# The first and the last group of a two-layer graph attention set apart: TensorE transposes at both ends, and the last output projection graph by graph

## Chip, cores, metric

The kernel runs on one core of one Trainium2 chip. The metric is the device time of one execution in microseconds. The runs of one kernel lie within some 0.3% of each other. "Span" is the time from the first to the last instruction in a profile; it is 1.5 to 2 us shorter than the device time of the same run. TensorE is called PE in the profile (PEld its weight loads), VectorE DVE, the scalar engine ACT, GpSimd POOL, and the DMA-issuing engine SP.

## The reference, cut to what matters

There are 128 graphs of 128 nodes with 512 features, all float32, and two attention layers with 8 heads.

```python
# layer 0                                             # layer 1
Q, K, V = x@W_q+b_q, x@W_k+b_k, x@W_v+b_v             q, k, v = x@Wq.T+bq, x@Wk.T+bk, x@Wv.T+bv
s = Q K^T / sqrt(64) + a_i + c_j + log(adj + 1e-9)    s = q k^T / sqrt(64) + log(clip(adj, 1e-8))
x = softmax(s) V + x                                  out = (softmax(s) v) @ Wo.T + bo
                                                      result = layer_norm(x + out) * gamma + beta
```

The initial gamma is all ones and beta all zeros.

## The kernel before

Four graphs form a group, and 32 groups pass through two layers, so there are 64 steps t. The products with the weights are one level of Strassen (seven products, P1 to P7, of four 128x256 matmuls each), computed in the order P1, P2, P6, P5, P7, P3 and P4 moved in between products of the next matrix. P6, P5 and P7 need sums of x (T1 to T4, made by GpSimd) and sums of the weights (S1 to S4, the "combine", made by VectorE). Work is put into numbered slots between the products; the order of the slots is the order of each engine's instructions in the program. In the profile's names p0, p1 and p2 are the PSUM banks into which TensorE writes the products, and the last letter is the matrix (P6 of V is `p0v<-wv,T`, P5 `p2v<-wv,T`); s are the scores, av the products with V, o the scalar engine's copy of av, aT its transpose, po the output projection, h what is normalised and stored. A record is one entry of the trace; a float32 matmul leaves two (four matmuls show as x8).

The matmuls take x transposed (`xT` in their records). It is loaded in 32x32 blocks; the DMA places the blocks and VectorE's stream transpose turns each block (0.71 us a graph):

```python
    load_tiles(0)
    strassen_weights(WV, 0, w_v0, "wv0", nc.scalar)
    load_graph(0, 0, nc.sync)       # 4 transfers of 64 KB each
    load_graph(0, 1, nc.sync)
    load_graph(0, 2, nc.scalar)
    load_graph(0, 3, nc.scalar)
    load_natural(0)                 # the same x again, as it lies, for the residual
    strassen_weights(WQ, 0, w_q0, "wq0", nc.scalar)
    strassen_weights(WK, 0, w_k0, "wk0", nc.scalar)
    load_adjacency(0, nc.sync)
    Strassen.combine(nc.vector, WV[0])
    for b in range(G):
        turn(XT[0][:, b])
```

The last group's output projection stands after everything else. Its operand is moved by DMA in blocks and turned by VectorE, for two graphs at a time:

```python
    for k in range(2):
        put(post, a + 5 + 4 * k, move, t, k, [nc.sync, nc.scalar] if k else [nc.sync])   # 16 transfers
    ...                                       # all slots run here
    for k in range(2):
        for b in (2 * k, 2 * k + 1):
            turn(AT[t][:, b])
        for b in (2 * k, 2 * k + 1):
            output(b)                         # 4 matmuls of 128x512, sum, statistics, scaling
            if b:
                finish(b - 1)                 # times gamma, plus beta, store
    finish(G - 1)
```

## Time and profile before

| | before |
|---|---|
| median of 3 runs | 3506.12 us (3505.57 to 3507.63) |
| span of the profiled run (another one, 3504.51 us) | 3502.7 us |
| PE busy | 3453.6 us |
| third product (P6) starts | 23.45 us |
| first scores' product of group 0 starts | 61.27 us |
| first scores' product of the last group starts | 3433.96 us |
| last instruction of any engine ends | 3496.6 us |

Read it by its two ends. Between the first scores' product and that of the last group TensorE has no gap to speak of (the longest between its records is 0.17 us), so any gain must come from before 61 us or after 3434 us. The prediction shows the lines.

### The profile page before, as it was taken

How to read it: one execution, taken by the hardware profiler on the slowest of the kernel's cores; microseconds unless marked ns; L12 is line 12 of the kernel's file. 1: busy time of each engine (PE TensorE's matmuls, PEld its weight loads, DVE VectorE, ACT ScalarE, POOL GpSimd, SP SyncE). 2: the span in 40 equal slices, each digit the busy share in tenths (PEclk: the TensorE clock that was granted, in tenths of full speed). 3: DMA queues.
4: the chain of work that ended last, by engine and by line, in shares of the span. 5: the costliest groups of instructions: out<-in, count | busy, mean ns of one | idle time of the engine just before them, and what ended most of it. 6: DMA issues, size and time to landing. Idle time of an engine off the chain costs nothing. (4 is left out here: it accounts for less than half of the span.)

```text
span 3502.7 us, 54508 instructions
## 1 busy us (share of the span) xinstructions
PE 3453.6 (99%) x20730; PEld 3080.4 (88%) x20730; DVE 1769.9 (51%) x2813; ACT 1203.0 (34%) x2333; POOL 1574.0 (45%) x987
## 2 busy tenths in 40 slices
PE   8999999999999999999999999999999999999996
PEld 7888888888888888888888888888888888888884
DVE  4555555555555555554444444545444444444443
ACT  2333333333333333333333333333333333333332
POOL 2333233333233333254555555555555555555554
PEclk9999999999999999999999999999999999999998
DMA  5332323332323332342333434242423333333432
GB/s 130 73 76 70 76 61 79 73 77 70 75 61 79 73 77 71 86 98 46 70 84 65 90 62 92 60 95 58 85 67 74 79 71 83 68 87 64 91 61 76
DMA packets 1036087, 265.33 MB, mean 76 GB/s; under 512 B 961840, under 2 KB 969008, under 8 KB 1035824
## 3 DMA queue, kind: packets, MB, share of 16 engines
q1 hardware_dynamic: 1026160, 257.86, 33.1%
q10 hardware_dynamic: 9664, 3.93, 0.5%
q8 instruction: 168, 2.75, 0.3%
q14 instruction: 95, 0.78, 0.1%
HBM read 160.97 MB, written 67.11 MB: 65 GB/s over the span
## 5 line engine op out<-in xcount | busy, mean ns | idle before, releaser
L99 PEld LDWEIGHTS av<-v,e 128*128 128x128 f32 x4096 | 537.3, 191 | 28.3 <-ACT o L99 1.8
L99 POOL TENSOR_TENSOR xn<-o,xn 128x1024 f32<-128x1024 f32 x64 | 148.8, 2324 | 862.6 <-DVE o L99 578.3
L99 PE MATMUL av<-v,e 128*128 128x65 f32 x4096 | 513.3, 268 | 1.4 <-ACT o L99 1.4
L99 DVE TENSOR_TENSOR e<-e,adjT 128x1024 f32<-128x1024 f32 x256 | 352.3, 1417 | 142.7 <-ACT e L99 142.7
L99 ACT COPY o<-av 128x260 f32<-128x260 f32 x512 | 192.6, 376 | 604.8 <-PE av L99 596.9
L99 POOL TENSOR_TENSOR xn<-xn,bo 128x1024 f32<-128x1024 f32 x64 | 153.6, 2419 | 368.5 <-DMA xn<-x1d 368.4
L99 POOL TENSOR_TENSOR T<-xT 128x512 f32<-128x512 f32 x128 | 208.7, 1631 | 188.2 <-DMA xn<-in_x_dram 105.0
L99 PE MATMUL p1v<-wv,T 128*128 128x256 f32 x1128 | 273.4, 385 | 0.0
L99 DVE SCALAR_TENSOR_TENSOR junk<-xn,wg 128x512 f32<-128x512 f32 x256 | 272.0, 1062 | 0.0
L99 PE MATMUL p0q<-T,wq 128*128 128x256 f32 x1128 | 268.3, 381 | 0.0
L99 PE MATMUL p1k<-T,wk 128*128 128x256 f32 x1128 | 266.5, 379 | 0.0
L99 PE MATMUL s<-qT,kT 64*128 64x128 f32 x4096 | 263.1, 278 | 0.0
L99 PEld LDWEIGHTS s<-qT,kT 64*128 64x128 f32 x4096 | 238.6, 188 | 25.6 <-issue 21.2
L99 DVE STREAM_TRANSPOSE xT<-xT 128x512 f32<-128x512 f32 x256 | 176.5, 700 | 156.8 <-DMA xT<-x1d 150.9
L99 PEld LDWEIGHTS p1k<-T,wk 128*128 128x128 f32 x1128 | 214.3, 190 | 29.1
L99 PEld LDWEIGHTS p0q<-T,wq 128*128 128x128 f32 x1128 | 211.7, 190 | 27.4
L99 PEld LDWEIGHTS p1v<-wv,T 128*128 128x128 f32 x1128 | 205.7, 190 | 25.4
L99 POOL TENSOR_TENSOR h<-h,xn 128x1024 f32<-128x1024 f32 x62 | 174.6, 2817 | 75.0 <-DVE h L99 75.0
L99 DVE TENSOR_TENSOR qT<-p2q,u3q 128x512 f32<-128x512 f32 x64 | 44.3, 692 | 312.3 <-ACT u3q L99 312.3
L99 ACT ACTIVATE e<-s,c 128x1024 f32<-128x1024 f32 x128 | 135.9, 1113 | 142.1 <-PE s L99 142.1
L99 PE MATMUL p0o<-wo,T_o 128*128 128x256 f32 x744 | 182.4, 388 | 0.0
L99 ACT ACTIVATE e<-s 128x1024 f32<-128x1024 f32 x128 | 124.1, 1021 | 142.1 <-PE s L99 142.1
(145 smaller groups left out, 6425.8 us busy)
## 6 DMA issues: line engine op xcount, KB each, us to landing
xn<-in_x_dram SPq DMA_DIRECT2D x64, 512.0 KB, 4.2
x1d<-xn SPq DMA_DIRECT2D x64, 512.0 KB, 3.0
xT<-x1d SPq DMA_DIRECT2D x512, 64.0 KB, 2.6
xn<-x1d SPq DMA_DIRECT2D x64, 512.0 KB, 6.3
aT<-o SPq DMA_DIRECT2D x1016, 32.0 KB, 2.0
xT<-in_x_dram SPq DMA_DIRECT2D x504, 64.0 KB, 2.7
out_dram<-h SPq DMA_DIRECT2D x62, 512.0 KB, 4.2
adjT<-in_adj_dram SPq DMA_DIRECT2D x256, 64.0 KB, 2.5
```

The lines of the kernel that those rows point to most:

```text
L99: return lambda *args, **kw: self.tc.keep_in_program_order(f(*args, **kw))
```

## The change

The intent is to take the block loads and block turning off the two places where nothing hides them. In the first group x is loaded only as it lies, ahead of the rest, and TensorE transposes it against an identity; wq and wk move to the sync queue. In the last group each graph is normalised, transposed on TensorE, projected and finished by itself, in the slots between the last products with V. The group before the last gets its statistics and scaling half by half, and VectorE takes gamma and beta of its second half over from GpSimd.

```diff
-    load_graph(0, 0, nc.sync) ... load_graph(0, 3, nc.scalar)
+    load_natural(0)
     strassen_weights(WV, 0, w_v0, "wv0", nc.scalar)
-    load_natural(0); strassen_weights(WQ ..., nc.scalar); strassen_weights(WK ..., nc.scalar)
     load_adjacency(0, nc.sync)
+    strassen_weights(WQ ..., nc.sync); strassen_weights(WK ..., nc.sync)
+    make_identity(nc, ident)
+    def transposed(dst, src, name, copy):
+        p = ps.tile([P, KC, N], F32, tag="s", bufs=2, ...)
+        for c in range(KC):
+            nc.tensor.transpose(p[:, c], src[:, c * P : (c + 1) * P], ident)
+        copy(dst, p)
+    for b in range(G):
+        transposed(XT[0][:, b], XN[0, b // 2][:, b % 2], ..., nc.vector.tensor_copy if b % 2 else nc.scalar.copy)
     Strassen.combine(nc.vector, WV[0])
-    for b in range(G):
-        turn(XT[0][:, b])
 ...
+                else:                                    # the group before the last
+                    for n in range(2):
+                        put(post, o - 1 + n, residual, t, n)
+                        ... stats, scales of this half at o + 1 + 2 * n
+                    ends = o + 2, o + 4
+                for n in range(2):
+                    put(post, ends[n], scale, t, 2 * n)
+                    put(post, ends[n], scale, t, 2 * n + 1)
+                    put(post, ends[n] + (t == LAST - 2), store, t, n, nc.vector if t == LAST - 2 and n else nc.gpsimd)
 ...
-    (move by DMA, turn, output and finish of the last group, as above)
+    for b in range(G):
+        put(post, a + 3 + 2 * b, normalise_one, b)
+        put(pre, a + 5 + 2 * b, transpose_one, b)
+        put(pre, a + 6 + 2 * b, output_one, b)
+        put(pre, a + 8 + 2 * b, finish_one, b)           # (h - mean) * rs; * gamma; + beta; store
```

More of the change, by code (lines that the diff above doesn't have):

```diff
@@ L425, in scale, with store @@
         nc.scalar.activation(h, h, AF.Identity, scale=rs[:, 0, b : b + 1], bias=rs[:, 1, b : b + 1])
-    def store(t, n):
+    def store(t, n, engine):
         _, g = split(t)
-        nc.gpsimd.tensor_tensor(HS[t, n], HS[t, n], wide(GA), ALU.mult)
-        nc.gpsimd.tensor_tensor(HS[t, n], HS[t, n], wide(BE), ALU.add)
+        engine.tensor_tensor(HS[t, n], HS[t, n], wide(GA), ALU.mult)
+        engine.tensor_tensor(HS[t, n], HS[t, n], wide(BE), ALU.add)
         nc.sync.dma_start(
@@ L452, in fast_path @@
     load_tiles(0)
+    load_natural(0)
     strassen_weights(WV, 0, w_v0, "wv0", nc.scalar)
-    load_graph(0, 0, nc.sync)
-    load_graph(0, 1, nc.sync)
-    load_graph(0, 2, nc.scalar)
-    load_graph(0, 3, nc.scalar)
-    load_natural(0)
-    strassen_weights(WQ, 0, w_q0, "wq0", nc.scalar)
-    strassen_weights(WK, 0, w_k0, "wk0", nc.scalar)
-    load_adjacency(0, nc.sync)
+    load_adjacency(0, nc.sync)
+    strassen_weights(WQ, 0, w_q0, "wq0", nc.sync)
+    strassen_weights(WK, 0, w_k0, "wk0", nc.sync)
+    ident = const.tile([P, P], F32, name="ident")
+    make_identity(nc, ident)
+    def transposed(dst, src, name, copy):
+        p = ps.tile([P, KC, N], F32, tag="s", name=f"tr_{name}", bufs=2, padded_shape=[P, 2 * KC, N])
+        for c in range(KC):
+            nc.tensor.transpose(p[:, c], src[:, c * P : (c + 1) * P], ident)
+        copy(dst, p)
+    for b in range(G):
+        transposed(XT[0][:, b], XN[0, b // 2][:, b % 2], f"x_{b}", nc.vector.tensor_copy if b % 2 else nc.scalar.copy)
+    TS[0] = quarters(XT[0])
     Strassen.combine(nc.vector, WV[0])
-    for b in range(G):
-        turn(XT[0][:, b])
-    TS[0] = quarters(XT[0])
     for s in Strassen.SUMS:
@@ L516, in fast_path @@
         put(pre, a + 3, scores, t, 1)
-        put(post, a + 5, normalise, t, 0)
-        put(post, a + 9, normalise, t, 1)
-        put(post, a + 9, count, t)
+        if t + 1 < LAST:
+            put(post, a + 5, normalise, t, 0)
+            put(post, a + 9, normalise, t, 1)
+            put(post, a + 9, count, t)
         if t:
@@ L555, in fast_path @@
                 o = slot("o", t, "P3")
-                for i, n in ((0, 1), (1, 0)):
-                    put(post, o + i, residual, t, n)
-                for i, b in enumerate((0, 1, 2, 3)):
-                    put(post, o + 3 + i, stats, t, b)
-                put(post, o + 6, scales, t, slice(0, G))
-                for i in range(2):
-                    put(post, o + 8 + i, scale, t, 2 * i)
-                    put(post, o + 8 + i, scale, t, 2 * i + 1)
-                    put(post, o + 8 + i, store, t, i)
+                if t < LAST - 2:
+                    for i, n in ((0, 1), (1, 0)):
+                        put(post, o + i, residual, t, n)
+                    for b in range(G):
+                        put(post, o + 3 + b, stats, t, b)
+                    put(post, o + 6, scales, t, slice(0, G))
+                    ends = o + 8, o + 9
+                else:
+                    for n in range(2):
+                        put(post, o - 1 + n, residual, t, n)
+                        for b in (2 * n, 2 * n + 1):
+                            put(post, o + 1 + 2 * n, stats, t, b)
+                        put(post, o + 1 + 2 * n, scales, t, slice(2 * n, 2 * n + 2))
+                    ends = o + 2, o + 4
[3 more added lines that the diff above has]
+                    put(post, ends[n] + (t == LAST - 2), store, t, n, nc.vector if t == LAST - 2 and n else nc.gpsimd)
     V1, V2 = slot("v", NG - 1, "P1"), slot("v", NG, "P1")
@@ L583, in fast_path @@
     a = slot("k", t, "P3") + 2
-    WR = {}
+    last = {}
     def plain_weight():
-        WR[0] = weights.tile([P, KC, D], F32, tag="w", name="wo_plain")
-        nc.sync.dma_start(WR[0], w_o1t.rearrange("(c p) e -> p c e", p=P))
-    put(post, slot("v", t, "P3"), plain_weight)
-    end = 7 * len(mats) + 3
-    for k in range(2):
-        put(post, a + 5 + 4 * k, move, t, k, [nc.sync, nc.scalar] if k else [nc.sync])
-    for i in range(-1, max(max(pre), max(post), end) + 1):
+        last["w"] = weights.tile([P, KC, D], F32, tag="w", name="wo_plain")
+        nc.sync.dma_start(last["w"], w_o1t.rearrange("(c p) e -> p c e", p=P))
@@ new lines, in prepare, with normalise_one @@
+    def prepare():
+        last["o"] = act.tile([P, G, D], F32, tag="xT", name="o_last", bufs=2)
+        AT[t] = act.tile([P, G, KC, N], F32, tag="aT", name="aT_last")
+        h = act.tile([P, G, D], F32, tag="xT", name="h_last", bufs=2)
+        HS[t, 0], HS[t, 1] = h[:, 0:2], h[:, 2:4]
+        RC[t] = small.tile([P, G, 2, KC], F32, tag="rc", name=f"rc_{t}", bufs=3)
+    def normalise_one(b):
+        o = OR[t, b // 2][:, b % 2]
+        rc = RC[t][:, b].rearrange("p s c -> p (s c)")
+        nc.vector.reciprocal(rc, o[:, :, HD])
+        nc.vector.tensor_tensor(
+            last["o"][:, b].rearrange("p (h d) -> p h d", d=HD), o[:, :, 0:HD],
+            rc.rearrange("p (h o) -> p h o", o=1).to_broadcast([P, H, HD]), ALU.mult,
+        )
@@ new lines, in transpose_one, with output_one @@
+    def transpose_one(b):
+        transposed(AT[t][:, b], last["o"][:, b], f"o_{b}", nc.scalar.copy if b % 2 else nc.vector.tensor_copy)
+    def output_one(b):
+        p = ps.tile([P, D], F32, tag=f"p{b % 3}", name=f"po_{t}_{b}")
+        for c in range(KC):
+            nc.tensor.matmul(p, AT[t][:, b, c], last["w"][:, c], start=(c == 0), stop=(c == KC - 1))
+        h = HS[t, b // 2][:, b % 2]
+        nc.vector.tensor_tensor(h, p, XN[t, b // 2][:, b % 2], ALU.add)
+        stats(t, b)
+        rs = RS[t][:, 0, b : b + 1]
+        nc.gpsimd.tensor_scalar_add(rs, MV[t][:, b, 1:2], LN_EPS)
+        nc.gpsimd.tensor_tensor(rs, rs, minus_half[:, b : b + 1], ALU.pow)
@@ new lines, in finish_one @@
+    def finish_one(b):
+        h = HS[t, b // 2][:, b % 2]
+        nc.vector.tensor_scalar(h, h, MV[t][:, b, 0:1], RS[t][:, 0, b : b + 1], ALU.subtract, ALU.mult)
+        nc.vector.tensor_tensor(h, h, GA, ALU.mult)
+        nc.vector.tensor_tensor(h, h, BE, ALU.add)
+        nc.sync.dma_start(out[split(t)[1] * G + b], h)
+    put(post, slot("v", t, "P3"), plain_weight)
+    put(post, a, prepare)
+    for b in range(G):
+        put(post, a + 3 + 2 * b, normalise_one, b)
+        put(pre, a + 5 + 2 * b, transpose_one, b)
+        put(pre, a + 6 + 2 * b, output_one, b)
+        put(pre, a + 8 + 2 * b, finish_one, b)
@@ L595, in fast_path @@
+    put(post, a + 9, count, t)
+    for i in range(-1, max(max(pre), max(post), 7 * len(mats) + 3) + 1):
         for u in pre.get(i, []):
@@ L600, in fast_path @@
             u()
-    for k in range(2):
-        HS[t, k] = work.tile([P, 2, D], F32, tag="h", name=f"h_{t}_{k}")
-    def output(b):
-        p = ps.tile([P, D], F32, tag=f"p{b % 3}", name=f"po_{t}_{b}")
-        for c in range(KC):
-            nc.tensor.matmul(p, AT[t][:, b, c], WR[0][:, c], start=(c == 0), stop=(c == KC - 1))
-        nc.vector.tensor_tensor(HS[t, b // 2][:, b % 2], p, XN[t, b // 2][:, b % 2], ALU.add)
-        stats(t, b)
-        scales(t, slice(b, b + 1))
-        scale(t, b)
-    def finish(b):
-        h = HS[t, b // 2][:, b % 2]
-        nc.vector.tensor_tensor(h, h, GA, ALU.mult)
-        nc.vector.tensor_tensor(h, h, BE, ALU.add)
-        nc.sync.dma_start(out[split(t)[1] * G + b], h)
-    for k in range(2):
-        for b in (2 * k, 2 * k + 1):
-            turn(AT[t][:, b])
-        for b in (2 * k, 2 * k + 1):
-            output(b)
-            if b:
-                finish(b - 1)
-    finish(G - 1)
 def layer_norm(nc, small, h, GA, BE, minus_half, name):
```

## The prediction

> **What bounds the kernel now.** I read the page's busy rows first, then the waits of TensorE, then windows over the two ends, then the order of instructions in time at each end, and last the chain that ended last.
>
> ```profile
> PE 3453.6 (99%) x20730; PEld 3080.4 (88%) x20730; DVE 1769.9 (51%) x2813; ACT 1203.0 (34%) x2333; POOL 1574.0 (45%) x987
> ...
> PE   8999999999999999999999999999999999999996
> ```
>
> TensorE is busy 99% of the span, and only the first and the last of the 40 slices are not full. So the kernel's length is TensorE's work plus what it stands idle at the ends. The waits say the same: four long ones carry nearly all of it.
>
> ```profile
> PE po L99 <- DVE aT L99: 17.1, 2, 13.4
> PE p0v L99 <- DVE xT L99: 11.5, 1, 11.5
> PE sums_total L662 <- DVE sums_ones L660: 6.8, 1, 6.8
> PE p0v L99 <- ACT t1v L99: 6.0, 1, 6.0
> ```
>
> The first and third are at the end, the second and fourth at the start. Windows over the ends (PE busy first, granted clock third from last):
>
> ```profile
> 18.40:23.40 5.00, 0.00 (x0) 0.00 (x0) 3.40 (x3) 1.87 (x2) 4.07 (x3) 0.95 1.16 286
> 23.40:30.00 6.60, 6.55 (x24) 5.61 (x25) 3.88 (x5) 0.59 (x1) 1.92 (x4) 0.78 0.90 215
> 30.00:87.00 57.00, 57.00 (x337) 50.86 (x336) 31.06 (x57) 18.98 (x38) 12.64 (x8) 1.00 0.42 83
> 3451.00:3469.00 18.00, 3.70 (x28) 3.15 (x27) 8.84 (x17) 4.43 (x8) 8.96 (x7) 0.66 0.28 47
> ```
>
> From 30 us on TensorE has no gap at all; in the 18 us from 3451 it works 3.7. The start in order of time:
>
> ```profile
> 18.45 0.71 DVE L99 STREAM_TRANSPOSE xT<-xT 128x512 f32<-128x512 f32 x1 [4.64 <-DMA wq<-in_L_gnn_W_q_dram]
> 19.25 1.26 POOL L99 TENSOR_TENSOR T<-xT 128x512 f32<-128x512 f32 x1 [18.81 <-DVE xT L99]
> ...
> 23.45 3.36 PE L99 MATMUL p0v<-wv,T 128*128 128x256 f32 x8 [5.97 <-ACT t1v L99]
> ...
> 26.64 1.89 PE L99 MATMUL p2v<-wv,T 128*128 128x256 f32 x8
> ```
>
> The fourth graph's x is turned only at 18.45 (the releaser named is wq, but what the instruction needs is the x load, issued on the same queue). GpSimd's sums T1 and T2 follow, then the third product, P6, at 23.4. In front of it only two products (P1, P2) have run, 3.4 us at the later pace of 1.72 us a product. The end in order of time:
>
> ```profile
> 3454.98 17.29 SPq L99 DMA_DIRECT2D aT<-o  x24
> ...
> 3468.74 1.31 DVE L99 STREAM_TRANSPOSE aT<-aT 128x512 f32<-128x512 f32 x2 [6.67 <-DMA aT<-o]
> 3469.51 9.22 PE L99 MATMUL po<-wo_plain,aT 128*128 128x512 f32 x16 [13.41 <-DVE aT L99]
> ...
> 3482.38 7.13 PE L99 MATMUL po<-wo_plain,aT 128*128 128x512 f32 x16 [3.65 <-DVE aT L99]
> ...
> 3496.49 0.14 DVE L663 TENSOR_SCALAR bad<-sums_total 1x1 int32<-1x1 f32 x1 [0.37 <-PE sums_total L662]
> ```
>
> The last product with V ends at 3456.1; the rows moved by DMA (32 transfers of 32 KB) hold the output projection back until 3469.5; the last instruction of any engine ends at 3496.6. So 40.5 us pass after the last product with V.
>
> [...] records of a 128x256 product take 634 ns at 11.5 us and 379 ns from about 15 us, and after the gap P6 needs 3.0 us where the next product needs 1.72. [...] o<-o,rc (128x1024) takes 1226 ns alone and 3311 ns beside GpSimd's residual; the four combines of wq take 5.67 us beside GpSimd's sums, those of wv alone 2.62.
>
> **The start, part by part.** Removed: 16 loads of x in 32x32 blocks (9.31 us of issuing on one queue and 9.91 on the other, which also held back the scalar engine's table load to 21.4 and with it the copy t1v) and four stream transposes. Added: 16 TensorE transposes and four copies out of PSUM; the identity is built by GpSimd, which is idle until x lands. The natural-layout x is loaded anyway; it moves to the front and costs two issues of 0.57 us.
>
> I work it out so. x (1 MB) and wv (1 MB) now go first, together. The slices of the DMA at the start show about 300 GB/s once running, from about 2 us: half of it, the first xn tile and half of wv, is there at 2 + 1.05 MB / 300 = 5.5, landed at about 6.3; all at about 9.3. A transpose I take at 0.25 us at full clock and 0.5 at half, from the 128x65 products with V (four in 1.00 us[...]): 1 to 2 us per graph. Graphs 0 and 1: 6.3 to about 9.5. Graphs 2 and 3: to about 12.5 (11 if one pass suffices, 14.3 if all stays cold). VectorE's copy of graph 3, 0.69: 13.2. GpSimd's T1 and T2, 1.3 each: 15.9. The combine of wv, which ran early before and now stands behind the copies, needs two operations for S2, 1.3 us alone and 2.8 beside GpSimd: 14.5 to 16. P1 and P2 run from 12.5, half cold, about 4.5 us: 17.0. So P6 starts at about 17.0, warm, and the product after it at 18.7 instead of 26.4. **Gain at the start: 7.7 us** (5.4 to 9.2). wq is needed at 22.2; it is issued on the one queue from about 7 and lands near 14. The loads of the second group move forward about as much as TensorE does, as the queue has 8 issues of x fewer.
>
> **The end, part by part.** I place everything on the clock of the kernel before. Up to av of graph 1 nothing moves. Graph 0 is normalised at 47.7 to 48.6 (3400 left off), transposed at 48.6 to 49.6, but its copy into aT waits for the last Strassen product that reads the old aT, which the transpose pushes to 51.3: copy 51.5 to 52.2, projection 52.3 to 54.0 (four matmuls of 0.43, warm). The two engines that set the rest are VectorE and, once, the scalar engine. The scalar engine has the scaling of the previous group's h ahead of the copy of av of graph 3; it waits for VectorE's statistics (57.9) and GpSimd's four small ones (1.7): 59.6, then two scales of 0.73 and the copy. As av has one bank, TensorE waits from 58.7 to about 61.7. Then transpose of graph 2 to 63.7, its copy 64.5, projection to 66.3; graph 3's transpose 67.3, copy behind another scaling 68.1, projection 69.8.
>
> VectorE is later than that. It has, after 63.8, copy 0.7, normalise 0.85, count 0.45, finish of graph 1 (0.5 + 1.4 + 1.4, beside GpSimd's gamma and beta of the previous group): 69.1; sum and statistics of graph 2, 1.5: 70.6; gamma and beta of 128x1024, which it took over from GpSimd, 1.7 + 1.2: 73.6; finish of graph 2, 1.9: 75.5; sum and statistics of graph 3, 1.5: 77.0; GpSimd's two small ones (0.9 to 1.7): 78.2; finish of graph 3, 1.9: 80.1; the good-count as before 0.84: 81.0. Before: 96.6. **Gain at the end: 15.6 us** (12 to 19). TensorE's own added work, 4 transposes of graphs and warm projections, lies in gaps or in the place of cold ones. What follows the last instruction (6.1 us, the landing of the last 256 KB among it) stays.
>
> **Sum.** 3506.1 - 7.7 - 15.6 = 3482.8, gain 0.66%.
>
> **Rivals.** (1) The first transposes don't warm the clock and run in two passes, and P1 and P2 are cold throughout: P6 at 19.3 or later, gain at the start 5, time 3486. [...] Against: P1 and P2 cold hide part of the wait for T2. (2) Loads set the start: xn is slower beside wv than I take it (in the steady state it lands in 4.2 us median, here with four wv transfers in the way), or wq on the sync queue arrives after 22. Each microsecond that xn lands later is one microsecond of the whole: 3484 to 3487. The early slices near 300 GB/s speak against. (3) Transposes among the products delay the scalar engine and TensorE stalls more than once on av's single bank; VectorE and GpSimd block each other longer than I take: gain at the end 11, time 3487. For it: 3311 against 1226 ns. (4) It goes better: [...] the start is limited only by the landing: gains 10 and 19, time 3477. (5) The long middle changes, through addresses of buffers that the identity shifts: its order of instructions is the same on each engine, and its windows show TensorE with no idle time, so nothing to win and little to lose; 0 expected.
>
> **Range and chances.** The rivals at their worst together give about 3491, at their best 3477. Run-to-run spread is 2 us. 8 in 10: 3476 to 3490. All idle time at both ends is about 20 (23.4 less two products) + 40.5 = 60 us, 1.7%; over 2% would need 70, which is not there to be won. To be slower by 2% a middle of 3400 us would have to change. So within 2% at 0.99.
>
> **What would show it.** Right: P6 (p0v<-wv,T) starts at 15.5 to 19 and the products behind it take 1.7 us; the waits of po on aT by DMA are gone; between the last product with V of graph 2 and that of graph 3 TensorE waits some 3 us for the scalar engine's o; the last instruction comes about 23 us sooner than before; the last chain is VectorE's h with little TensorE; the middle's products keep 379 ns. Wrong: P6 later than 20, or waiting for wv's combine or wq; a gap at the second group's first product; the end's VectorE idle rather than busy in the last 15 us, which would say that the scalar engine or GpSimd sets it; a middle whose windows show idle TensorE.

That a transpose takes as long as a product with V (0.25 us) was the estimate from the 1.00 us of four such products. No term of the sum is cut: it came to 3506.1 - 7.7 - 15.6 = 3482.8 us. Its half clock is the 0.50 granted in the trace of before from 3456.70 to 3473.70 us; its passes are the two records of a float32 matmul; that VectorE and GpSimd "block each other" means that o<-o,rc took 1226 ns alone and 3311 ns beside GpSimd's residual, and in the changed kernel's trace GpSimd's rs<-mv (128x1) 0.22 and 0.23 us alone and 1.10 us beside VectorE's gamma of 128x1024.

## The result, and the profile after

The changed kernel takes 3484.1 us, the median of 4 runs (3483.54 to 3484.22), against 3505.85 us (3504.56 to 3507.63) before. The ratio is 0.9937, 95% interval 0.9920 to 0.9955. Ratios here and below are the mean time of one kernel's runs over the mean of the other's of the same rounds, so they are not quite the ratios of the medians quoted. The gain of 0.6% is well clear of the spread.

The page of the changed kernel, the same two lines:

```profile
PE 3456.8 (99%) x20762; PEld 3083.9 (89%) x20762; DVE 1778.8 (51%) x2819; ACT 1200.5 (34%) x2333; POOL 1569.2 (45%) x983
...
PE   9999999999999999999999999999999999999998
```

TensorE's work is the same within 3.2 us, while the span fell from 3502.7 to 3482.4. The first slice is now full. Its waits (us in total, times, longest):

```profile
PE sums_total L694 <- DVE sums_ones L692: 7.8, 1, 7.8
PE tr_x L99 <- DMA xn<-in_x_dram: 5.8, 1, 5.8
PE av L99 <- ACT o L99: 2.1, 1, 2.1
PE p1q L99 <- DVE v L99: 1.8, 1, 1.8
```

The 17.1 us that the projection po waited for aT by DMA, and the 11.5 and 6.0 us of the start, are gone. Two waits are new: p1q, the first product of Q, waits for VectorE's v, and av, a product with V, waits for the scalar engine's copy o. The start in order of time (start, length, engine, operation, in brackets the idle time before it and its releaser):

```profile
5.77 1.94 PE L99 MATMUL tr_x<-ident,xn 128*128 128x128 f32 x8 [5.77 <-DMA xn<-in_x_dram]
...
11.11 5.70 DVE L99 TENSOR_TENSOR wv<-wv 128x512 f32<-128x512 f32 x4
...
14.64 1.99 PE L99 MATMUL p0v<-wv,T 128*128 128x256 f32 x8
...
16.47 1.89 PE L99 MATMUL p2v<-wv,T 128*128 128x256 f32 x8
...
21.13 0.68 DVE L99 TENSOR_TENSOR v<-p1v,t1v 128x512 f32<-128x512 f32 x1
...
21.86 1.99 PE L99 MATMUL p1q<-xT,wq 128*128 128x256 f32 x8 [1.77 <-DVE v L99]
```

P6 starts at 14.64 in place of 23.45, and the product after it 10.2 us sooner than before. Then 1.8 us are given back: the first product of Q needs the PSUM bank p1, which VectorE's add into v frees, and this add stands in VectorE's order behind the combines of wv and wq. The combine of wv took 2.62 us before, in VectorE's idle time at 7.9 us; now it runs beside GpSimd's sums and takes 5.70. The first scores' product starts at 53.14 in place of 61.27. **Against this trace of before the start gives 8.1 us.** One trace is not enough here: the old start brings the first scores' product at 59.58 in e_tail below, which leaves 6.4 us, and a second profile of the changed kernel (e_after below) has P6 at 15.56 but the scores at 53.24, as the wait in front of Q takes up the difference (1.1 us there).

Then the lead stays at 8.13 us until about 2000 us, where it grows by 0.44: the profiled run of before had one late adjacency load there. It is 8.62 us at the last group. The end of the changed kernel:

```profile
3453.10 1.52 ACT L99 ACTIVATE h<-h,rs 128x512 f32<-128x512 f32 x2 [4.23 <-POOL rs L99]
...
3454.93 1.35 PE L99 MATMUL av<-v,e 128*128 128x65 f32 x8 [2.12 <-ACT o L99]
...
3457.80 2.36 POOL L99 TENSOR_TENSOR h<-h,gamma 128x1024 f32<-128x1024 f32 x1
...
3457.92 5.94 PE L99 MATMUL po<-wo_plain,aT_last 128*128 128x512 f32 x8 [0.78 <-DVE aT_last L99]
3458.01 2.69 DVE L99 TENSOR_TENSOR o_last<-o,rc 128x512 f32<-128x512 f32 x1
...
3460.23 2.67 POOL L99 TENSOR_TENSOR h<-h,beta 128x1024 f32<-128x1024 f32 x1
3460.62 2.32 DVE L99 TENSOR_SCALAR ok<-rc 128x32 f32<-128x32 f32 x1
...
3476.72 0.15 DVE L695 TENSOR_SCALAR bad<-sums_total 1x1 int32<-1x1 f32 x1 [0.45 <-PE sums_total L694]
```

The last instruction ends 51.5 us after the last group's first scores' product (3425.34); in the trace of before it was 62.7. Against that trace the end gives 11.1 us. Three things stand out in it: the wait for the scalar engine (2.1 us), two VectorE instructions that last longer beside GpSimd's gamma and beta (2.69 in place of 0.69, and 2.32 in place of 0.17), and the projection of graph 2, 5.94 us where those of graphs 0, 1 and 3 take 3.7. Windows over this stretch give the reason for the last (length, busy time of each engine, then the clock granted to TensorE, third from the right):

```profile
3443.00:3453.00 10.00, 9.77 (x38) 5.21 (x37) 9.43 (x17) 1.34 (x3) 5.58 (x7) 1.00 0.00 0
3453.00:3457.90 4.90, 2.21 (x12) 1.81 (x12) 3.70 (x9) 2.18 (x5) 2.32 (x8) 0.77 0.14 54
3457.90:3463.90 6.00, 5.98 (x10) 2.64 (x11) 5.90 (x7) 1.49 (x2) 4.92 (x2) 0.62 0.01 3
```

The granted clock was 0.77 over the stretch with the gaps before it (2.1 and 0.8 us, TensorE busy 2.21 of 4.90 us) and 0.62 while it ran: it was 0.50 from 3455.63 to 3462.46 us and full again after that. No gap of TensorE between 3443 us and this fall was over 2.2 us. But this slow projection costs the changed kernel nothing yet, as VectorE comes to it later: the sum of graph 2 follows VectorE's own work at 3465.01 without a wait. In the trace of e_combine below the same projection takes 3.70 us, as the other three do at full clock,

```profile
3455.23 3.70 PE L99 MATMUL po<-wo_plain,aT_last 128*128 128x512 f32 x8 [0.78 <-DVE aT_last L99]
```

and the end is as long as that of e_after, where it is slow (50.9 us both).

### The profile page after: what moved, and what is told of

Same layout as the page of the kernel before. It is cut to its first block, busy times and chain, and to the rows that moved or that the text cites. A ratio compares the mean times of both kernels' runs of the same rounds, so it can differ in the third digit from the quotient of the medians.

```text
span 3482.4 us, 54486 instructions
## 1 busy us (share of the span) xinstructions
PE 3456.8 (99%) x20762; PEld 3083.9 (89%) x20762; DVE 1778.8 (51%) x2819; ACT 1200.5 (34%) x2333; POOL 1569.2 (45%) x983
## 4 chain that ended last, share of the span: by engine, by line
PE 98%; DVE 1%; DMA 0%; POOL 0%; issue 0%; ACT 0%; ACTq 0%; DVEq 0%
PE av L99 12%; PE p1v L99 11%; PE p0q L99 10%; PE p1k L99 10%; PE s L99 7%; PE p0o L99 6%; PE p2q L99 6%; PE p2v L99 6%; PE p2k L99 6%; PE p1q L99 6%; PE p0v L99 6%; PE p0k L99 6%; PE p2o L99 3%; PE p1o L99 2%; DMA wv<-in_L_gnn_W_v_dram 0%; DVE h_last L99 0%
```

## The experiments

Twelve runs were made, one of them the changed kernel again; all gave the right result. Those of one call share the chip and the runs of the kernel before.

| run | median us | before, same call | ratio (95%) |
|---|---|---|---|
| e_head | 3498.98 | 3506.74 | 0.9977 (0.9960 to 0.9994) |
| e_tail | 3491.33 | 3506.74 | 0.9958 (0.9941 to 0.9975) |
| e_queue | 3507.05 | 3506.74 | 1.0002 (0.9986 to 1.0019) |
| e_combine | 3481.76 | 3506.74 | 0.9930 (0.9914 to 0.9947) |
| e_after | 3484.01 | 3506.58 | 0.9937 (0.9921 to 0.9954) |
| e_port | 3481.89 | 3506.58 | 0.9931 (0.9914 to 0.9947) |
| e_both | 3482.79 | 3506.58 | 0.9934 (0.9917 to 0.9951) |
| e_act | 3483.01 | 3506.58 | 0.9935 (0.9918 to 0.9951) |
| e_best | 3477.57 | 3507.31 | 0.9917 (0.9904 to 0.9931) |
| e_keep | 3477.65 | 3507.31 | 0.9917 (0.9904 to 0.9931) |
| e_warm_t, e_warm_m | 3481.70, 3482.78 | 3507.31 | one run each, state unknown |

The intervals reach some 5 to 6 us to either side, more than most of the runs differ: the kernel before lies between 3505.11 and 3512.85 in the first call, 3503.40 and 3507.43 in the second, 3504.08 and 3508.74 in the third, and each new kernel within 3 us. So gains against the kernel before are not known to better than a few us; kernels of one call can be held against each other more closely, by their own runs.

### Each end alone: e_head and e_tail

```diff
 e_head: the kernel before with the changed start only
 e_tail: the changed kernel with the old start (and the identity built after it)
```

> Only the start is changed (x in natural layout first, transposes on TensorE, weights' queue); the end stays as before. If the two parts add up, as the traces say (the first scores' product starts 8.1 us sooner in the changed kernel), this is 8.1 us under the kernel before, 3497.7 us. Rival: the parts overlap or part of the gain comes from the middle or from the shifted buffers; then it is off by more than 1.5 us.

> Only the end is changed, the start stays as before. Theory: the rest of the difference, about 11.7 us from the last scores' product on, so 3494.2 us. Rival, the recorded prediction's term of 15.6 us: 3490.3 us.

Measured: e_head is 7.8 us under the kernel before and e_tail 15.4 us, by the medians. Together 23.2, and the changed kernel in the next call is 22.6 under. By the intervals of the ratios the two gains are only known as 2 to 14 us and 9 to 21 us. So the two ends add up as far as this can tell, and the buffers shifted by the identity cost nothing that shows. But e_tail is not the 3494.2 that the two traces promised; it is near the prediction's own term. Its end is just as long as in the changed kernel (51.5 us). What differs is the old end: in e_head it takes 66.1 us and in e_queue 66.2, where the trace of before had 62.7. The second pair of projections tells why (2.8 of the 3.4 us in e_head). First before, then e_head (windows around that pair; granted clock third from the right):

```profile
3482.40:3490.00 7.60, 7.12 (x16) 2.94 (x16) 3.80 (x7) 0.81 (x1) 2.10 (x6) 1.00 0.09 36
```

```profile
3474.50:3484.50 10.00, 9.91 (x16) 4.05 (x16) 3.43 (x7) 0.81 (x1) 1.85 (x4) 0.72 0.07 26
```

The same 16 records take 7.1 us at full clock in one and 9.9 us at 0.72 in the other. The old end leaves TensorE idle for 13.4 us and then, for 3.65 us, in front of the second pair. In e_head the granted clock was 0.59 over the start of the first pair (3461.00 to 3467.70), 0.91 from there to 3474.50 and 0.72 over the second pair, so it came back during the first pair and fell again about the second gap; in e_queue the second pair took as long (9.95 us). In the one trace of before it was 0.64 from 3469.00 to 3475.50 and then 1.00 to the end of the second pair: it did not fall there, though the gap is the same. So three traces of this end show two outcomes, and that of before was the good one (the section on e_best and e_keep says what differs). The old start scatters too: P6 started at 23.45 us in before and at 21.49 in e_tail.

### Which part of the start: e_queue

```diff
-    strassen_weights(WQ, 0, w_q0, "wq0", nc.scalar)
-    strassen_weights(WK, 0, w_k0, "wk0", nc.scalar)
+    strassen_weights(WQ, 0, w_q0, "wq0", nc.sync)
+    strassen_weights(WK, 0, w_k0, "wk0", nc.sync)
```

> The kernel before, with the loads of wq and wk on the sync queue in place of the scalar one. Rival theory of the start: what held it up was the scalar engine's queue (its table load and the copy t1v came only at 21.4 us behind twelve and more issues), not the 32x32 blocks and their turning; then P6 starts as early as 15 to 18 us and the time falls by 5 us or more. Own theory: the fourth graph's x lands no sooner, GpSimd's T2 is ready at about 21.8 us as before, so P6 moves from 23.4 to about 22 and the time falls by 1.6 us at most, 3504.3 us.

Measured: no gain in time (3507.05 against 3506.74). In its trace P6 starts at 22.19, and what it waits for is no longer the scalar engine:

```profile
22.19 3.78 PE L99 MATMUL p0v<-wv,T 128*128 128x256 f32 x8 [4.34 <-POOL T L99]
```

So the copy t1v behind the scalar engine's queue, which the profile of before named as the 6.0 us wait, was only the last of two. With it taken away GpSimd's T2 ends the wait 1.3 us sooner, and T2 hangs on the fourth graph's block loads, which are turned at 18.41 (18.45 before). At the first scores' product 0.3 us of it are left (60.93 against 61.27), and the time shows none; so the rival falls, and the 1.6 us that I allowed did not come either. The gain of the start belongs to the loads and transposes, not to the queue alone. No run separates the loads in one piece from the transposes on TensorE.

### The wait given back at the start: e_combine

```diff
-    put(post, 2, lambda: Strassen.combine(nc.vector, WQ[0]))
+    put(post, 6, lambda: Strassen.combine(nc.vector, WQ[0]))
```

> The changed kernel with the combine of wq four units later on VectorE. Theory: the first product of Q (P1) waits 1.8 us for VectorE's add into v, which frees the PSUM bank and stands behind the combines of wv and wq; with the second combine moved, P1 of Q follows P7 of V with no gap and the time falls by 1.8 us, to 3482.3 us. Rival: the bias or wq itself came late, or the wait comes back at the product that needs the combined wq; then no gain, 3484 us.

Measured: 3481.76 us, 2.3 under the changed kernel's 3484.01 to 3484.1. In its trace the first scores' product of the last group starts at 3423.32 in place of 3425.34, 2.0 us sooner, and Q follows V without a gap:

```profile
18.22 1.89 PE L99 MATMUL p0v<-wv,T 128*128 128x256 f32 x8
18.29 0.67 DVE L99 TENSOR_TENSOR v<-p1v,t1v 128x512 f32<-128x512 f32 x1
19.94 1.89 PE L99 MATMUL p1q<-xT,wq 128*128 128x256 f32 x8
```

The theory holds: it was the order on VectorE (the rest of the 2.3 is within the scatter), and the wait does not come back at the products with the combined wq.

### What sets the end: e_after, e_port, e_both, e_act

e_after is the changed kernel again, as the measure for the other three.

> The changed kernel itself once more, as the measure for the others of this call. 3484 us; its tail, from the last but one scores' product to the last instruction, 51.5 us as in its first profile and in the run of the end alone, while the kernels with the old end show 62.7 to 66.2 us, by whether TensorE's clock was back for the second pair of projections or not. If the new end is that steady, its times lie within 1 us of each other.

Measured: 3484.01 (3483.74 to 3484.29), as steady as expected. Its end takes 50.9 us, 0.6 less than in the first profile. There the instructions that last longer beside GpSimd are others (the second count instruction, 2.33 us, and in the finish of graph 1 the product with gamma, 2.73): which one is hit changed between two profiles of one kernel, the total is about the same.

```diff
 e_port: store(t, 0) of the group before the last without its two GpSimd instructions (right only as gamma is 1 and beta 0)
 e_both: the same two on VectorE, one slot later
-    put(post, ends[n] + (t == LAST - 2), store, t, n, nc.vector if t == LAST - 2 and n else nc.gpsimd)
+    put(post, ends[n] + (2 - n if t == LAST - 2 else 0), store, t, n, nc.vector if t == LAST - 2 else nc.gpsimd)
 e_act: scaling of that half behind the copy of av on the scalar engine
-                    ends = o + 2, o + 4
+                    ends = o + 3, o + 4
```

> The changed kernel without GpSimd's gamma and beta on the first half of the last but one group (gamma is ones and beta zeros in these inputs, so the result stays right). Theory: these two instructions hold VectorE up by 4.0 us (normalise of graph 3 and the count take 5.3 us in place of 1.3), but the projection of graph 2 (5.9 us at the low clock, ending at 3463.9) then takes their place, so only 0.9 to 1.5 us are won: 3482.9 us. Rival, the block is what sets the end: 4 us are won, 3480.1 us.

> These two instructions on VectorE (2.4 us) ahead of the normalise of graph 3, none on GpSimd. Theory: VectorE has 3 us to spare there before the projection of graph 2 ends, so it is as without them, 0.9 to 1.5 us won, 3482.9 us. Rival: VectorE's work in order sets the end, so 4.0 - 2.4 = 1.6 us are won: 3482.5 us. These two lie too close to tell apart by time; the trace tells: theory expects VectorE's sum of graph 2 to wait for TensorE.

> The changed kernel with the scaling of the last but one group's first half behind the copy of graph 3's first product with V on the scalar engine. Theory: TensorE's wait of 2.1 us for that copy goes, the transpose of graph 2 comes 2 us sooner, its copy 1.1 us sooner (VectorE is busy until then): 1.1 us won, and up to 2.5 if the clock stays up for the projection of graph 2: 3482.0 us. Rival, as the prediction put it, VectorE alone sets the end and the scalar engine's order matters nothing: 3484 us.

Measured: e_port is 2.1 us under e_after, e_both 1.2, e_act 1.0, by the medians. In e_port's trace the stretched instructions are short, and a new wait is there:

```profile
3458.00 0.17 DVE L99 TENSOR_SCALAR ok<-rc 128x32 f32<-128x32 f32 x1
...
3462.73 0.69 DVE L99 TENSOR_TENSOR h_last<-po,xn 128x512 f32<-128x512 f32 x1 [2.41 <-PE po L99]
```

Of the 4 us or so that GpSimd's two instructions cost VectorE, 2.4 turn into a wait for the projection of graph 2, which is slow here too (5.40 us in place of 3.70). That is what the theory said, if a little more than its 0.9 to 1.5 us, and the rival (all 4 are won) falls by the median; but the four runs lie between 3480.30 and 3483.09, and the one at 3480.30 is where the rival put it. It was not traced; whether its projection ran at full clock is not known. By their traces the ends of e_port and e_both last 49.2 and 49.6 us, against 50.9; the 0.9 us by which their times differ is within what one profile and a few runs can tell. In e_both the trace was to decide, and it goes against the theory, if barely: the sum of graph 2 does not wait for TensorE. It starts at 3462.68, straight after the finish of graph 1, and the projection had ended 0.04 us before, so VectorE's own work and the slow projection are as long as each other there. In e_act TensorE's wait for o is gone, and the wait now stands before the projection of graph 2 (2.65 us for VectorE's copy). The gain is about the 1.1 us expected for the order alone (the 3482.0 us needed the clock to stay up as well, and the projection took 5.20 us); the rival, that the scalar engine's order matters nothing, falls, if only by 1 us.

### Together, and TensorE's gap filled: e_best and e_keep

```diff
 e_best = e_combine + e_act + both halves' gamma and beta on VectorE, and
-        nc.vector.tensor_scalar(h, h, mean, rs, ALU.subtract, ALU.mult)
-        nc.vector.tensor_tensor(h, h, GA, ALU.mult)
-        nc.vector.tensor_tensor(h, h, BE, ALU.add)
+        nc.vector.scalar_tensor_tensor(h, h, mean, GA, op0=ALU.subtract, op1=ALU.mult)
+        nc.vector.scalar_tensor_tensor(h, h, rs, BE, op0=ALU.mult, op1=ALU.add)
 e_keep = e_best with three idle matmuls of 128x512 between transpose and projection of graph 2
```

> What the runs so far point to, together: the combine of wq later (2.0 us at the start), the scaling behind the copy on the scalar engine (1.1), gamma and beta of the last but one group on VectorE (1.5), and the finish of a graph in two VectorE instructions in place of three, the first of which needs only the mean and so does not wait for GpSimd's power (0.5 us for each of three graphs and the 1.0 us wait of the last). Sum 2.0 + 1.1 + 1.5 + 2.5 = 7.1: 3477 us, and in its trace the sum of graph 2 waits for TensorE's projection at the low clock. Rival: the parts hide one another and it stays above 3479 us.

> The same with three projections of 128x512 for nothing in TensorE's gap between the transpose and the projection of graph 2 (2.6 us of work in a gap of 2.7). Theory: the projection of graph 2 takes 5.2 to 5.9 us because the clock falls in the gaps; filled, it takes 3.5 to 3.7 us, VectorE's work then sets the end and 0.6 us more are won: 3476.4 us. Rival: the projection is slow for another reason (its operands, the new bank); then it takes 5 us still and nothing is won.

Measured: e_best takes 3477.57 us (3477.35 to 3478.09), 6.4 to 6.5 under the changed kernel's medians, against 7.1 expected. It beats both kernels. In its trace the end gives 5.0 us (46.5 against 51.5, with 5.1 expected) and the start 1.5 of the 2.0. One part of the expectation is a miss: I expected the sum of graph 2 to wait for a slow projection, but in e_best that projection runs at full clock (3.70 us) without any filling, and VectorE is the bound. So e_keep had nothing to mend (3477.65), and it can't tell what it was made for. The same gap with two outcomes, in e_act and then in e_best:

```profile
3456.73 5.20 PE L99 MATMUL po<-wo_plain,aT_last 128*128 128x512 f32 x8 [2.65 <-DVE aT_last L99]
```

```profile
3455.16 3.70 PE L99 MATMUL po<-wo_plain,aT_last 128*128 128x512 f32 x8 [2.61 <-DVE aT_last L99]
```

The gap before the projection is 2.6 us in both; in one the clock fell, in the other not. The times at which the clock changed differ in one thing. In the traces of before and of the changed kernel they lie whole multiples of 3.41 us apart (before: it falls at 3456.68, returns at 3473.74 and falls at 3494.22; changed: 3455.63, 3462.46 and 3472.70), and where these steps begin differs between the two. Take e_act and e_best in steps of the same length, placed by their own clock records (e_act falls at 3456.37). In e_act the gap (3454.08 to 3456.73) lies almost whole in one step; in e_best (3452.55 to 3455.16) a boundary at 3453.98 cuts it in two. First e_act's step, then the first of the two in e_best (busy time of TensorE first):

```profile
3452.96:3456.37 3.41, 1.12 (x11) 0.89 (x9) 3.27 (x9) 1.78 (x3) 1.08 (x4) 1.00 0.20 77
```

```profile
3450.56:3453.98 3.42, 1.99 (x14) 1.39 (x12) 3.06 (x7) 1.78 (x3) 1.38 (x3) 1.00 0.20 77
```

The second step of e_best has TensorE busy for 2.23 us. After the step with 1.12 us the clock fell, after 1.99 and 2.23 it did not. The old end fits: in e_head one step holds most of the 3.65 us gap (busy 0.97 us, and the clock fell), in before it is cut into steps with 1.58 and 1.60 us busy, and the clock stayed. So does the changed kernel (the step before the fall at 3455.63 has 1.29 us). That points to where the steps lie; no run moved the steps or the gap on purpose, so it is not shown, and busy time alone does not sort the cases: among the products with V the clock fell after a step with 2.48 us in e_head (the next four matmuls took 1.97 us in place of 1.11), and in before it fell after one with 2.21.

### Do transposes count for the clock: e_warm_t and e_warm_m

```diff
+    warm = ps.tile([P, KC, N], F32, tag="p2", name="warm")
+    for i in range(20):                                              # e_warm_m: 10, with
+        nc.tensor.transpose(warm[:, i % KC], ident, ident)           # nc.tensor.matmul(..., ident, ident)
```

> The changed kernel with 20 transposes of the identity for nothing in TensorE's wait for the first x, from about 1.4 to 6.2 us. If transposes count for the clock, as the early full clock in the changed kernel (P2 of V at 1.9 us a product, 7 us after the first transpose) lets one think, the transposes of graphs 2 and 3 take 0.5 us a graph in place of 1.0 and P1 of V takes 1.9 us in place of 2.6 to 2.9. If they do not count[...] these stay at 1.0 and 2.6 to 2.9. The time: 3484 us either way, within 1 us, as VectorE's combine sets the start.

> The same with 10 matmuls of the identity with itself in place of the 20 transposes, the same time on TensorE by the records so far. These surely count: P1 of V at 1.9 us, transposes of graphs 2 and 3 at 0.5 us. If it looks like the run with transposes, transposes count as matmuls do. 3484 us.

Both are single runs of unknown state, so only their traces are used. The transposes of the first two graphs and the first product P1 of V, with idle transposes ahead (e_warm_t), then with idle matmuls (e_warm_m):

```profile
1.35 4.50 PE L99 MATMUL warm<-ident 128*128 128x128 f32 x20 [1.35 <-POOL ident L99]
...
5.67 1.06 PE L99 MATMUL tr_x<-ident,xn 128*128 128x128 f32 x8
...
8.54 1.89 PE L99 MATMUL p0v<-wv,xT 128*128 128x256 f32 x8
```

```profile
5.79 1.24 PE L99 MATMUL tr_x<-ident,xn 128*128 128x128 f32 x8
...
8.77 1.89 PE L99 MATMUL p0v<-wv,xT 128*128 128x256 f32 x8
```

Eight transposes take 1.06 us in place of 1.94, and P1 takes 1.89 in place of 2.55. That is not scatter: three traces with the new start and no idle work ahead (the changed kernel, e_head, e_combine) have 1.94 us for the eight transposes each time and 2.55, 2.86 and 2.82 for P1. So 20 idle transposes from 1.35 us on brought the clock up as 10 idle matmuls did: after the matmuls the eight transposes took 1.24 us and P1 1.89. In the changed kernel's trace, without idle work, the records of P1 still start at 634 ns and come down to 379 ns. All of this is float32; no run here has another type. A transpose's record took 421 ns (median) in the changed kernel's start and 273 ns in its end, where four of them took 0.60 us, so the records follow each other by 0.11 us. The expectation on the time was wrong on the good side, by the traces: GpSimd's T2 and VectorE's combine start sooner as well, so P6 starts at 12.88 in place of 14.64. That this would add to e_best was not tried.

## Why the prediction was right, and where its terms were off

The mechanism held: both ends lose the waits that were named, each end alone gains, and the middle stays as it was. The sum came out as well: 3482.8 predicted, 3484.1 measured, two ends of 7.7 and 15.6 us against 7.8 and 15.4 by the medians of each end alone. That it is so close is luck: several terms were off and partly cancel, and the intervals of the timed runs are wider than the agreement.

| term of the prediction | predicted | measured (changed kernel's trace) |
|---|---|---|
| first x landed | 6.3 us | 5.8 |
| four transposes of a graph, low clock | 1 to 2 us | 1.0 |
| the last of them done | 12.5 us | 10.5 |
| P6 / the product after it | 17.0 / 18.7 us | 14.6 / 16.5 |
| wait of the first product of Q | none | 1.8 us |
| gain at the start | 7.7 us | 8.1 |
| four transposes at full clock (end) | 1.0 us | 0.42 (their weight loads) |
| projection of one graph | 1.7 us | 3.7, and 5.9 at the low clock |
| four small GpSimd instructions before the scaling | 1.7 us | 2.7 |
| TensorE's wait for the av bank | 3.0 us | 2.1 |
| normalise of graph 3 and count | 1.3 us | 5.3 |
| finish of graph 1 | 3.3 us | 1.9 |
| last group's first scores' product to the last instruction | 47.0 us | 51.5 |

The start. The loads were placed well; x landed 0.5 us sooner, and the transposes were over-estimated (one record each, where a float32 matmul has two), so P6 came 2.4 us sooner than said (1.4 in e_after's trace). This did not come through, as the prediction did not follow the add into v: it gave the combine of wv a share beside GpSimd only as far as S2 and overlooked that all of VectorE's work behind it, and so the bank p1, moves too. e_combine shows that this wait is worth 2.0 us. Three of its readings are off a little: 379 ns is reached at 16.2 us, not at about 15; the product after P6 started at 26.64, as its own line shows, not at 26.4; and the 16 loads of x did not by themselves hold the table load to 21.4, as in e_queue, with wq and wk off that queue, it comes at 11.78.

The end. The term "four matmuls of 0.43" for a projection was misread: 0.43 us is one record, and a float32 matmul of 128x512 has two, as the 7.13 us of the old second pair (two graphs) could have told. It cost little as VectorE was later than TensorE, as the prediction said. That VectorE's instructions last longer beside GpSimd's was foreseen but put too low: in this trace it fell on the normalise and the count (5.3 us against 1.3), not on the finish of graph 1 (1.9 against 3.3); in e_after's on the count and the finish. Together the three took 7.2 us in place of 4.6. That the clock would fall again in the new end was not foreseen; taking GpSimd's two instructions away (e_port) leads straight to that slow projection. Altogether the new end is 4.5 us longer than predicted.

That the total came out nevertheless has a reason which the prediction could not see from one trace: the profiled run of before had its second pair of projections at full clock. Against that trace the new end gains 11.1 us; against the two other traces of the old end (66.1 and 66.2 us) it gains 14.6 us. So an old end 3.5 us longer in other runs made up for a new end 4.5 us longer than worked out. For the same reason the sum mixes two runs: its terms are read from a run of 3504.51 us and taken off a median of 3506.12.

Its signs. The waits on aT by DMA are gone and the middle has no gap, as said. P6 was to start at 15.5 to 19 and started at 14.64 (15.56 in e_after's trace); TensorE was to wait some 3 us for the scalar engine's o and waited 2.1; the last instruction was to come about 23 us sooner and came 19.8 sooner, against the one trace.

The rivals. Rival 1 (transposes do not warm the clock) falls by e_warm_t (1.06 us for eight transposes in place of 1.94). Rival 2 (loads are late) did not come: x was there at 5.8 us and wq in time. Rival 3 (stalls on av's bank, VectorE longer beside GpSimd) is what happened in kind, at about the size given by it when held against the trace of before. Rival 4 (gains of 10 and 19 us) did not come. Rival 5 held: the middle did not change but for 0.44 us of one late load in the trace of before.

## What to carry to other kernels

Where a pipelined kernel is full in its middle, gains lie in the fill and the drain, and there a route that costs TensorE and the copying engines more (transposes on TensorE with copies out of PSUM) can beat the one that is hidden inside. Here it did at both ends (7.8 and 15.4 us); at the last group it came together with the finishing graph by graph, and no run tells how much each of the two gave. When work moves from an idle stretch onto a shared engine, follow everything that stands behind it in that engine's order, not only the operand you think of: the wait that came back here was for a PSUM bank (1.8 us). And take more than one trace of a stretch in which TensorE idles: after the same gap of 3.65 us its clock was up in one trace here and down in another (7.1 and 9.9 us for the same matmuls).
